# Two attention blocks in one kernel: sums of exponentials and divisors formed on column quarters, their inverses spread by way of DRAM

## The chip, the core and the metric

One core of a Trainium2 chip runs the whole program. The time is device time in microseconds (us), from the median of three runs: 2657.57 before the change (2656.48 to 2659.49). The profile is of one execution; in it the engines are PE (TensorE, matrix products), DVE (VectorE), ACT (ScalarE), POOL (GpSimd) and SP (which only issues transfers).

## What is computed

The input x has 8 images of 512 channels and 4096 pixels (64 x 64), all in float32. Two attention blocks follow each other.

Block 0, for each image:

```
f = Wf x + bf                      (64 x 4096)
g = pool2x2(Wg x + bg)             (64 x 1024)
v = pool2x2(Wh x + bh)             (256 x 1024)
s = f^T g ; beta = softmax(s)      (4096 x 1024, along the 1024)
o = v beta^T                       (256 x 4096)
x1 = gamma (Wv o + bv) + x
```

Block 1, on x1:

```
q = delu(Wq x1 + bq), k = delu(Wk x1 + bk)      (64 x 4096 each)
delu(z) = 10 relu(z) + exp(10 min(z, 0))
KV = k (Wv1 x1 + bv1)^T                         (64 x 512)
norm[n] = 1 / sum_d q[d, n] (sum_n k[d, n] + 1e-10)
out = x1 + gamma1 (KV^T q) norm
```

Two divisors matter here. The softmax of block 0 divides column n of the exponentials by their sum over 1024 rows. Block 1 divides column n of q by `norm`'s sum. Both are one number per pixel, while the data that they divide has pixels along the free dimension and something else on the 128 partitions. So the inverse is needed as a row that stands on every partition.

## The kernel before

Pixels are taken in chunks of 512 columns (`CH`), 8 per image, 64 in all (`TOTAL`). The function `step(s)` handles chunk s of the attention, and along with it work of other chunks, in three strands:

- A, for chunk a = s + 9: the products fg (L259) and, in a scheme of seven instead of eight partial products, H (L303), with pooling on DVE. POOL forms the sums of x that H needs (L292 to L295) and DVE the results.
- The attention of chunk s: M (L484, seven products with the exponentials E), N (L547, the output projection, added into the chunk of x called xb), and pk (L593, the features q and k of block 1). For chunk s + 1 the step computes the scores s (L394), their exponentials on ACT (L398), the sums over them on DVE (L432 to L437), the total (L441), its inverse (L446) and the normalized E (L460).
- C, for the image before (`b_c`), on pairs of chunks: `normalize` forms the divisors pd (L770), inverts them (L774) and multiplies q by the inverse (L777); `finish` forms pa (L795), copies it to y on ACT (L798), and POOL issues a transfer that adds y to the output in DRAM (L801). Two pa groups of 1 MB make up a pair. `normalize` runs on steps with j = 0, 1, 3, 5 of an image, `finish` on odd ones.

The order of the work on every engine is written by hand. Each piece is entered with `at(t, function, ...)`, t being a place within the step on a scale of about 41; the pieces are sorted by t and their instructions issued in that order on each engine's queue (`manual_schedule`). A place is not a time: an engine runs its queue in order as fast as its waits allow.

The total of the exponentials is a product with a matrix of ones: all 128 partitions of the result hold the same row of 512 sums. DVE inverts all of it. pd is made in the same way with the matrix kb, whose two diagonal blocks of 64 x 64 hold the sum of k in each row, so that partitions 0 to 63 hold the divisors of one chunk of the pair and partitions 64 to 127 those of the other.

PSUM is used as 8 banks that go round (`bank`), SBUF scratch as 7 buffers (`scratch`). A product enters PSUM in two matmul instructions[...].

A check runs alongside: `look` (L450, L451) sums the totals and inverses into chk; at the end DVE compares them with a limit and every engine reads the outcome. If it failed, the program would run once more in a general form; in these runs it does not.

SP issues the loads of x (L212, L224), the stores of xb (L574), the transposing transfers of v, x and k (u and uv; L358, L648, L630), and at the end the loads and stores of the last image, which takes another path for C.

Of the kernel before, what the change touches and what calls it, by code (L numbers as in the profile page):

```python
# [36 lines left out]
F32 = mybir.dt.float32  # L37
U16 = mybir.dt.uint16
AF = mybir.ActivationFunctionType
ALU = mybir.AluOpType  # L40
AX = mybir.AxisListType

PARAM = 10.0
EPS = 1e-10
P = 128
CH = 512
SAFE = 1e27

# [2 lines left out]
def tile_two_attention_blocks(  # L51
# [21 lines left out]
    nc = tc.nc  # L73
    B, C, H, W = x.shape
    N = H * W
    D = WfT.shape[1]
    CV = WhT.shape[1]
    KT = C // P
    VT = CV // P
    NCHUNK = N // CH  # L80
    M = N // 4
    MT = M // P
    NT = CH // P
    TOTAL = B * NCHUNK
    HN = CH // 2
    xr = x.rearrange("b (k p) h w -> b p k (h w)", p=P)
    outr = out.rearrange("b (k p) h w -> b p k (h w)", p=P)
    wv1r = wvT.rearrange("(k p) o -> p k o", p=P)

    const = ctx.enter_context(tc.tile_pool(name="const", bufs=1))  # L90
# [23 lines left out]
    for e in range(2):  # L114
        nc.scalar.dma_start(out=b_kq[e * D : (e + 1) * D, e : e + 1], in_=bk.rearrange("(p o) -> p o", o=1))
        nc.scalar.dma_start(
            out=b_kq[(1 - e) * D : (2 - e) * D, e : e + 1], in_=bq.rearrange("(p o) -> p o", o=1)
# [6 lines left out]
    ident = const.tile([P, P], F32, name="ident")  # L124
# [4 lines left out]
    ones = const.tile([P, P], F32, name="ones")  # L129
    nc.gpsimd.memset(ones, 1.0)  # L130

    kk = const.tile([P, CH], F32, name="kk")

    kb = const.tile([P, P], F32, name="kb")
# [28 lines left out]
    chk = const.tile([P, 2, TOTAL], F32, name="chk")  # L163

    def half(e):
        return slice(e * D, (e + 1) * D)

    def run(ctx, general):
# [6 lines left out]
        work1 = ctx.enter_context(tc.tile_pool(name="work1", bufs=1))  # L175
        work = ctx.enter_context(tc.tile_pool(name="work", bufs=2))
        temp = ctx.enter_context(tc.tile_pool(name="temp", bufs=7))
        turned = ctx.enter_context(tc.tile_pool(name="turned", bufs=1))
        small = ctx.enter_context(tc.tile_pool(name="small", bufs=4))
        psum = ctx.enter_context(tc.tile_pool(name="psum", bufs=8, space=bass.MemoryType.PSUM))  # L180

        def bank(name):
            return psum.tile([P, CH], F32, tag="m", name=name)

        def scratch(name):
            return temp.tile([P, CH], F32, tag="t", name=name)

# [38 lines left out]
        st = {}  # L226
        fgs, fs, vps = {}, {}, {}

        th, hs, es, sums, totals, rtots, te, os_, to, ns = ({} for _ in range(10))
        pxs, x_last, stored, late = [], {}, {}, {}  # L230
        kTs, xTs, pks, qq, halves, turned_halves = ({} for _ in range(6))

# [195 lines left out]
        def sum_of_e(s, m):  # L428
# [6 lines left out]
            else:  # L435
                r = sums[s]
                nc.vector.tensor_tensor(r[:, 0, :], r[:, 0, :], r[:, 1, :], ALU.add)  # L437

        def total(s):
            pt = totals[s] = bank(f"tot_{s}")  # L440
            nc.tensor.matmul(pt, ones, sums[s][:, 0, :], start=True, stop=True)  # L441

        def invert(s):

            rtots[s] = bank(f"rtot_{s}")
            nc.vector.reciprocal(rtots[s], totals[s])  # L446

        def look(s):
            pt = totals[s]
            nc.scalar.activation(pt, pt, AF.Copy, accum_out=chk[:, 0, s : s + 1])  # L450
            nc.scalar.activation(pt, rtots[s], AF.Copy, accum_out=chk[:, 1, s : s + 1])  # L451

        def block(s, i, j):

# [309 lines left out]
        def normalize(pair, at, t, t_invert, t_out):  # L764

            m = {}

            def product():
                m["pd"] = bank(f"pd_{pair}")
                nc.tensor.matmul(m["pd"], kb, qq[pair], start=True, stop=True)  # L770

            def inversion():
                m["rn"] = scratch(f"rn_{pair}")
                nc.vector.reciprocal(m["rn"], m["pd"])  # L774

            def out():
                nc.vector.tensor_tensor(qq[pair], qq[pair], m["rn"], ALU.mult)  # L777

            at(t, product)
            at(t_invert, inversion)  # L780
            at(t_out, out)

        def finish(pair, ks, at, t):

            b, jp = divmod(pair, NCHUNK // 2)
            m = {}

            def product():
                kv = st[b]["kv"]
                y = m["y"] = yc.tile([P, 2, 2, CH], F32, tag="y", name=f"y_{pair}_{ks[0]}")  # L790
                for i, k in enumerate(ks):
                    for e in range(2):
                        pa = bank(f"pa_{pair}_{k}_{e}")
                        hf = half(1 - e)
                        nc.tensor.matmul(  # L795
                            pa, kv[hf, bass.ts(k, P)], qq[pair][hf, :], start=True, stop=True
                        )
                        nc.scalar.copy(y[:, i, e, :], pa)  # L798

            def out():  # L800
                nc.gpsimd.dma_start(  # L801
                    out=outr[b, :, ks[0] : ks[0] + 2, bass.ts(jp, 2 * CH)],
                    in_=m["y"].rearrange("p k e n -> p k (e n)"), accum_op=ALU.add,
                )

            at(t, product)
            at(t + 3.4, out)


        def place(s, *tiles):  # L810
# [82 lines left out]
        def step(s):  # L893
            here, after = 0 <= s < TOTAL, 0 <= s + 1 < TOTAL
            a = s + LEAD
# [3 lines left out]
            pair = (b_c * NCHUNK + j) // 2  # L899
            work = []  # L900

            def at(t, fn, *args):
                work.append((t, len(work), fn, args))
# [50 lines left out]
                    turn_G(b_c, at, 19.5)  # L954
                    make_KV(b_c, at, 21.4, 30.0)
            if c_here and here and j == 0:
                normalize(pair, at, 5.6, 6.9, 13.2)
            if c_here and here and j % 2 == 1 and j < NCHUNK - 1:
                normalize(pair + 1, at, 3.5, 4.9, 4.95)
            if c_here and here and j % 2 == 1:  # L960
                finish(pair, (0, 1), at, 9.2)
                finish(pair, (2, 3), at, 10.9)
            if 0 <= a < TOTAL:
                a_h(a, at, 19.7, 29.1, 38.2 if here else 36.9, 38.4 if here else 37.8)

# [17 lines left out]
            if after:  # L983
                n = s + 1
                if here:
                    at(5.7, weigh_two, n, 0)
                    at(7.5, weigh_two, n, 2)
                    for m, t in ((2, 9.3), (4, 10.6), (6, 11.8), (8, 13.1)):
                        at(t, sum_of_e, n, m)

                if not here:
                    t, t_invert = 21.2, 21.25
                elif s == 0:
                    t, t_invert = 21.2, 22.6
                else:
                    t, t_invert = 16.1 if j % 2 == 1 and c_here else 17.85, 18.0
                at(t, total, n)
                at(t_invert, invert, n)
                if not general:
                    at(max(21.5, t_invert + 0.1), look, n)  # L1000
                at(24.3, normalize_block, n, 0, 1)
                at(26.0, normalize_block, n, 0, 0)
                at(27.3, normalize_block, n, 1, 1)
                at(29.2, normalize_block, n, 1, 0)
                at(33.6, sums_of_e, n, 1)
                at(36.0, sums_of_e, n, 2)
# [65 lines left out]
        for s in range(-LEAD, TOTAL + 1):  # L1072
            step(s)
# [5 lines left out]
    with ExitStack() as stack, tc.manual_schedule(engines=ENGINES):  # L1079
        run(stack, general=False)  # L1080

    least = const.tile([1, 1], F32, name="least")
    good = const.tile([1, 2 * TOTAL], F32, name="good")
    nc.vector.tensor_scalar(good, chk[0:1].rearrange("p c s -> p (c s)"), SAFE, None, ALU.is_lt)
    nc.vector.tensor_reduce(least, good, AX.X, ALU.min)
    bad = const.tile([1, 1], mybir.dt.int32, name="bad")
    nc.vector.tensor_scalar(bad, least, 0.5, None, ALU.is_lt)
    again = nc.values_load(bad, min_val=0, max_val=1, skip_runtime_bounds_check_because="0 or 1")
    with tc.If(again > 0):
        with ExitStack() as stack, tc.manual_schedule(engines=ENGINES):  # L1090
            run(stack, general=True)
# [37 lines left out]
```

## Time and profile before

| what | value |
|---|---|
| median of three runs | 2657.57 us |
| the profiled execution | 2656.62 us, span 2654.5 us, granted clock 0.994 |
| total L441: matmul instructions | 128, 66.1 us busy |
| divisors pd L770: matmul instructions | 56, 29.3 us busy |
| DVE reciprocal L446, 128 x 512 | 64, mean 3365 ns |
| DVE reciprocal L774, 128 x 512 | 28, mean 3351 ns |
| accumulating transfers L801 | 56 of 1 MB, 8.3 to 17.6 us to landing, median 11.4 |
| from total to total in the middle of an image | 39.3 and 40.2 us in turn (pa and pd stand in the longer one; on odd steps the total stands one M product earlier) |

The page gives busy time of each engine as a share of the span. A matmul's own duration includes its way through the array, so the time that it costs is read from start to start of neighbours in the timeline. An idle time stands with the group that ended it, and the entry behind the arrow names what it waited for. "Landing" is the time from a transfer's issue to its completion.

### The profile page before, as it was taken

What the parts mean: (1) busy time and instruction counts of PE and PEld (TensorE: products, weight loads), DVE (VectorE), ACT (ScalarE), POOL (GpSimd) and SP (SyncE); (2) the same over time, 40 slices, a digit from 0 to 9 for tenths busy, and PEclk for the clock granted to TensorE, in tenths of its full rate; (3) what the DMA queues carried; (4) which work ended last, traced back from release to release, by engine and by line L of the source; (5) the groups of instructions that cost most, each with busy time, mean ns of one, the idle gap of its engine ahead of it and who ended that gap; (6) DMA issues with size and microseconds to landing.
All of it is one profiled execution on the core that took longest, in us unless ns stands there. A gap on an engine that the chain in (4) does not pass through costs nothing.

```text
span 2654.5 us, 30415 instructions
## 1 busy us (share of the span) xinstructions
PE 2606.4 (98%) x10650; PEld 1798.1 (68%) x10650; DVE 2136.8 (80%) x2990; ACT 1593.2 (60%) x2670; POOL 763.5 (29%) x610
## 2 busy tenths in 40 slices
PE   8899999999999999999999999999999999999996
PEld 6577666667667667667667676666676676666663
DVE  5788879878888878887888888888788788798873
ACT  3365566566566566575675665666665656756661
POOL 4422323322322323223333223323223232221112
PEclk9999999999999999999999999999999999999998
DMA  5143455465555565655664654756555656455657
GB/s 172 49 134 89 115 135 149 104 164 134 133 157 118 142 167 118 164 133 116 152 162 121 155 125 123 180 116 151 141 118 158 155 119 159 117 138 138 154 144 256
DMA packets 465363, 369.91 MB, mean 139 GB/s; under 512 B 339888, under 2 KB 340400, under 8 KB 465200
## 3 DMA queue, kind: packets, MB, share of 16 engines
q1 hardware_dynamic: 444816, 307.16, 42.6%
q0 software_dynamic: 15232, 58.72, 12.0%
q10 hardware_dynamic: 5152, 1.97, 0.3%
q8 instruction: 87, 1.43, 0.2%
q14 instruction: 76, 0.62, 0.1%
HBM read 151.92 MB, written 134.22 MB: 108 GB/s over the span
## 4 chain that ended last, share of the span: by engine, by line
PE 87%; DVE 6%; DMA 1%; issue 1%; ACT 1%; POOL 0%; SPq 0%; DVEq 0%; POOLq 0%; ACTq 0%
PE M L484 27%; PE N L547 14%; PE H L303 11%; PE s L394 8%; PE pk L593 7%; PE fg L259 7%; PE pg L687 4%; PE pa L795 3%; PE tot L441 2%; PE pkv L752 1%; PE pd L770 1%; DMA xb<-in_x_dram 1%; DVE T L469 1%; DVE T L466 1%; DVE r L434 0%
## 5 line engine op out<-in xcount | busy, mean ns | idle before, releaser
L560 POOL TENSOR_TENSOR xb<-xb,n 128x512 f32<-128x512 f32 x192 | 246.7, 1285 | 553.3 <-ACT n L557 504.2
L484 PEld LDWEIGHTS M<-T,S 128*128 128x128 f32 x1536 | 286.5, 190 | 114.3 <-issue 29.2
L557 ACT ACTIVATE n<-N,gb_v 128x256 f32<-128x256 f32 x384 | 161.2, 471 | 334.1 <-PE N L547 333.2
L484 PE MATMUL M<-T,S 128*128 128x256 f32 x1536 | 358.7, 383 | 0.0
L655 ACT COPY xT<-u 128x1024 uint16<-128x1024 uint16 x252 | 328.2, 1353 | 1.4
L460 DVE TENSOR_TENSOR E<-E,rtot 128x1024 f32<-128x1024 f32 x256 | 305.2, 1214 | 3.8 <-issue 1.6
L642 ACT COPY w<-xb 128x1024 uint16<-128x1024 uint16 x252 | 244.8, 1042 | 81.8 <-DVE xb L563 81.8
L398 ACT ACTIVATE E<-s 128x512 f32<-128x512 f32 x512 | 256.1, 615 | 48.3 <-PE s L394 40.6
L446 DVE RECIPROCAL rtot<-tot 128x512 f32<-128x512 f32 x64 | 215.3, 3365 | 49.4 <-PE tot L441 49.4
L547 PE MATMUL N<-to,w_v 128*128 128x256 f32 x1024 | 243.6, 381 | 3.2 <-ACT n L557 3.0
L563 DVE TENSOR_TENSOR xb<-xb,N 128x512 f32<-128x512 f32 x256 | 175.0, 684 | 84.2 <-POOL xb L560 81.9
L394 PE MATMUL s<-f,g 64*128 64x512 f32 x1024 | 238.1, 602 | 1.9 <-DVE o L493 1.9
L593 PE MATMUL pk<-xb,w_kqk 128*128 128x512 f32 x512 | 231.8, 595 | 8.0 <-DVE xb L568 8.0
L634 POOL COPY kT<-uk 128x512 uint16<-128x512 uint16 x56 | 53.1, 949 | 620.6 <-DMA uk<-wk 620.6
L484 PE MATMUL M<-E,vT 128*128 128x256 f32 x1024 | 231.5, 379 | 0.0
L450 ACT ACTIVATE tot<-tot 128x512 f32<-128x512 f32 x64 | 37.7, 589 | 320.0 <-DVE rtot L446 319.9
L547 PEld LDWEIGHTS N<-to,w_v 128*128 128x128 f32 x1024 | 194.3, 191 | 30.8 <-ACT n L557 4.4
L484 PEld LDWEIGHTS M<-E,vT 128*128 128x128 f32 x1024 | 194.6, 190 | 29.4 <-issue 1.9
L259 PE MATMUL fg<-xa,w_fg 128*128 128x512 f32 x472 | 213.9, 596 | 0.0
L547 PE MATMUL N<-o,w_v 128*128 128x256 f32 x768 | 187.7, 380 | 1.9 <-ACT n L557 1.9
L547 PEld LDWEIGHTS N<-o,w_v 128*128 128x128 f32 x768 | 145.1, 190 | 54.8 <-issue 24.2
L394 PEld LDWEIGHTS s<-f,g 64*128 64x128 f32 x1024 | 94.7, 186 | 116.5 <-issue 90.6
(149 smaller groups left out, 4647.8 us busy)
## 6 DMA issues: line engine op xcount, KB each, us to landing
xb<-in_x_dram SPq DMA_DIRECT2D x64, 1024.0 KB, 5.7
out_dram<-xb SPq DMA_DIRECT2D x64, 1024.0 KB, 5.3
xa<-in_x_dram SPq DMA_DIRECT2D x59, 1024.0 KB, 7.4
out_dram<-y POOLq DMA_DIRECT2D x56, 1024.0 KB, 11.4
w_v<-in_L_conv_wv_dram SPq DMA_DIRECT2D x8, 1024.0 KB, 8.1
x_early<-in_x_dram SPq DMA_DIRECT2D x4, 1024.0 KB, 5.7
u<-w SPq DMA_TRANSPOSE x252, 3.3
x<-out_dram SPq DMA_DIRECT2D x12, 256.0 KB, 10.7
```

What stands on the lines that cost most here:

```text
L259: nc.tensor.matmul(fg, w_fg[:, k, :], x_a[a][:, k, :], start=(k == 0), stop=(k == KT - 1))
L303: nc.tensor.matmul(m[i], w_h7[i][:, k, :], th[a][i][:, k, :], start=(k == 0), stop=(k == hk - 1))
L394: nc.tensor.matmul(sc[e], g[half(e), i, :], fs[s][half(e), :], start=True, stop=True)
L398: nc.scalar.activation(es[s][:, 2 * i + e, :], sc[e], AF.Exp)
L446: nc.vector.reciprocal(rtots[s], totals[s])
L460: nc.vector.tensor_tensor(b, b, r, ALU.mult)
L484: nc.tensor.matmul(m[i], v7[i][:, k, :], te[s][i][:, k, :], start=(k == 0), stop=(k == hm - 1))
L547: nc.tensor.matmul(a[:, k, :], w_v7[i][:, bass.ts(k, P)], b, start=not more and k == 0, stop=True, skip_group_check=more or k > 0,)
L560: nc.gpsimd.tensor_tensor(of_x(*ij), of_x(*ij), u, ALU.add)
L593: nc.tensor.matmul(pk, w_kqk[:, i, e * D : (e + 2) * D], x_b[s][:, i, :], start=(i == 0), stop=(i == KT - 1),)
L642: nc.scalar.copy(w, x_b[s][:, k, :].bitcast(U16).rearrange("p (n h) -> p h n", h=2))
L655: nc.scalar.copy(v[:, k], u)
```

## The change

- `total` for s from 2 to 55 uses 32 columns of the ones for each of four column quarters of 128. Each quarter's sums land on their own 32 partitions of one PSUM tile of 128 x 128. DVE inverts that tile into SBUF (`rq`).
- `spread_inverses` sends one partition of each quarter to a row of DRAM and loads that row back, repeated on all 128 partitions; `keep_inverses` has ACT copy it into a PSUM bank, which the normalization reads as before. The first two chunks and those of the last image keep the full product.
- `product` of `normalize` uses 32 columns of kb around its middle, so that each quarter's 32 partitions hold 16 rows of each chunk's divisors. `inversion` inverts 128 x 128, sends eight rows to DRAM and loads them back on 64 partitions each, in two transfers.
- Both inverted tiles share the tag `rq` with one buffer. The transfers are SP's; they stand ahead of the transposing transfer of v (18.7) on its queue.
- The places of C: product, inversion and multiplication at 12.65, 13.7 and 30.9. The accumulating transfers go to 22.6 and 22.7, behind POOL's sums of x. On step 55 (`a == TOTAL`) both groups of pa stand at 21.4 and 22.3, behind the last M and ahead of N.
- On step 55 the total stands at 21.2, inverted at 22.6; on later even steps at 19.55 and 19.6.
- The check at the end covers all 128 partitions of chk, with a transpose and a second reduction.

```diff
@@ -43,6 +43,7 @@
 PARAM = 10.0
 EPS = 1e-10
 P = 128
+QP = 32
 CH = 512
 SAFE = 1e27
 
@@ -177,6 +178,7 @@
         temp = ctx.enter_context(tc.tile_pool(name="temp", bufs=7))
         turned = ctx.enter_context(tc.tile_pool(name="turned", bufs=1))
         small = ctx.enter_context(tc.tile_pool(name="small", bufs=4))
+        rows = ctx.enter_context(tc.tile_pool(name="rows", bufs=2, space=bass.MemoryType.DRAM))
         psum = ctx.enter_context(tc.tile_pool(name="psum", bufs=8, space=bass.MemoryType.PSUM))
 
         def bank(name):
@@ -226,7 +228,7 @@
         st = {}
         fgs, fs, vps = {}, {}, {}
 
-        th, hs, es, sums, totals, rtots, te, os_, to, ns = ({} for _ in range(10))
+        th, hs, es, sums, totals, rq, rtots, te, os_, to = ({} for _ in range(10))
         pxs, x_last, stored, late = [], {}, {}, {}
         kTs, xTs, pks, qq, halves, turned_halves = ({} for _ in range(6))
 
@@ -436,19 +438,45 @@
                 r = sums[s]
                 nc.vector.tensor_tensor(r[:, 0, :], r[:, 0, :], r[:, 1, :], ALU.add)
 
+        def by_quarters(s):
+
+            return 1 < s < TOTAL - NCHUNK
+
         def total(s):
-            pt = totals[s] = bank(f"tot_{s}")
-            nc.tensor.matmul(pt, ones, sums[s][:, 0, :], start=True, stop=True)
+            if not by_quarters(s):
+                totals[s] = bank(f"tot_{s}")
+                nc.tensor.matmul(totals[s], ones, sums[s][:, 0, :], start=True, stop=True)
+                return
+
+            pt = totals[s] = bank(f"tot_{s}")[:, 0:P]
+            for i in range(NT):
+                nc.tensor.matmul(
+                    pt[bass.ts(i, QP), :], ones[:, 0:QP], sums[s][:, 0, bass.ts(i, P)],
+                    start=True, stop=True,
+                )
 
         def invert(s):
-
-            rtots[s] = bank(f"rtot_{s}")
-            nc.vector.reciprocal(rtots[s], totals[s])
+            if by_quarters(s):
+                rq[s] = work1.tile([P, P], F32, tag="rq", name=f"rq_{s}")
+            else:
+                rq[s] = rtots[s] = bank(f"rtot_{s}")
+            nc.vector.reciprocal(rq[s], totals[s])
+
+        def spread_inverses(s):
+
+            d = rows.tile([NT, P], F32, tag="rd", name=f"rd_{s}")
+            nc.sync.dma_start(out=d, in_=rq[s][0:P:QP, :])
+            u = rtots[s] = scratch(f"rb_{s}")
+            nc.sync.dma_start(out=u, in_=d.rearrange("(o i) n -> o (i n)", o=1).to_broadcast([P, CH]))
+
+        def keep_inverses(s):
+            u, rtots[s] = rtots[s], bank(f"rtot_{s}")
+            nc.scalar.copy(rtots[s], u)
 
         def look(s):
             pt = totals[s]
             nc.scalar.activation(pt, pt, AF.Copy, accum_out=chk[:, 0, s : s + 1])
-            nc.scalar.activation(pt, rtots[s], AF.Copy, accum_out=chk[:, 1, s : s + 1])
+            nc.scalar.activation(pt, rq[s], AF.Copy, accum_out=chk[:, 1, s : s + 1])
 
         def block(s, i, j):
 
@@ -766,12 +794,26 @@
             m = {}
 
             def product():
-                m["pd"] = bank(f"pd_{pair}")
-                nc.tensor.matmul(m["pd"], kb, qq[pair], start=True, stop=True)
+
+                pd = m["pd"] = bank(f"pd_{pair}")[:, 0:P]
+                for i in range(NT):
+                    nc.tensor.matmul(
+                        pd[bass.ts(i, QP), :], kb[:, D - QP // 2 : D + QP // 2],
+                        qq[pair][:, bass.ts(i, P)], start=True, stop=True,
+                    )
 
             def inversion():
-                m["rn"] = scratch(f"rn_{pair}")
-                nc.vector.reciprocal(m["rn"], m["pd"])
+                rd = work1.tile([P, P], F32, tag="rq", name=f"rq_pd_{pair}")
+                nc.vector.reciprocal(rd, m["pd"])
+                d = rows.tile([2 * NT, P], F32, tag="rn", name=f"rn_{pair}_row")
+                nc.sync.dma_start(out=d, in_=rd[0 : P : QP // 2, :])
+                rn = m["rn"] = scratch(f"rn_{pair}")
+                for e in range(2):
+                    row = d.rearrange("(i e) n -> e i n", e=2)[e : e + 1]
+                    nc.sync.dma_start(
+                        out=rn[half(e)].rearrange("p (i n) -> p i n", n=P),
+                        in_=row.to_broadcast([D, NT, P]),
+                    )
 
             def out():
                 nc.vector.tensor_tensor(qq[pair], qq[pair], m["rn"], ALU.mult)
@@ -780,7 +822,7 @@
             at(t_invert, inversion)
             at(t_out, out)
 
-        def finish(pair, ks, at, t):
+        def finish(pair, ks, at, t, t_out):
 
             b, jp = divmod(pair, NCHUNK // 2)
             m = {}
@@ -804,7 +846,7 @@
                 )
 
             at(t, product)
-            at(t + 3.4, out)
+            at(t_out, out)
 
 
         def place(s, *tiles):
@@ -954,12 +996,14 @@
                     turn_G(b_c, at, 19.5)
                     make_KV(b_c, at, 21.4, 30.0)
             if c_here and here and j == 0:
-                normalize(pair, at, 5.6, 6.9, 13.2)
+                normalize(pair, at, 12.65, 13.7, 30.9)
             if c_here and here and j % 2 == 1 and j < NCHUNK - 1:
-                normalize(pair + 1, at, 3.5, 4.9, 4.95)
+                normalize(pair + 1, at, 12.65, 13.7, 30.9)
             if c_here and here and j % 2 == 1:
-                finish(pair, (0, 1), at, 9.2)
-                finish(pair, (2, 3), at, 10.9)
+
+                cover = a == TOTAL
+                finish(pair, (0, 1), at, 21.4 if cover else 9.2, 24.9 if cover else 22.6)
+                finish(pair, (2, 3), at, 22.3 if cover else 10.9, 25.8 if cover else 22.7)
             if 0 <= a < TOTAL:
                 a_h(a, at, 19.7, 29.1, 38.2 if here else 36.9, 38.4 if here else 37.8)
 
@@ -990,12 +1034,17 @@
 
                 if not here:
                     t, t_invert = 21.2, 21.25
-                elif s == 0:
+                elif s == 0 or a == TOTAL:
                     t, t_invert = 21.2, 22.6
+                elif a > TOTAL and s % 2 == 0:
+                    t, t_invert = 19.55, 19.6
                 else:
                     t, t_invert = 16.1 if j % 2 == 1 and c_here else 17.85, 18.0
                 at(t, total, n)
                 at(t_invert, invert, n)
+                if by_quarters(n):
+                    at(18.01, spread_inverses, n)
+                    at(23.0, keep_inverses, n)
                 if not general:
                     at(max(21.5, t_invert + 0.1), look, n)
                 at(24.3, normalize_block, n, 0, 1)
@@ -1079,12 +1128,16 @@
     with ExitStack() as stack, tc.manual_schedule(engines=ENGINES):
         run(stack, general=False)
 
-    least = const.tile([1, 1], F32, name="least")
-    good = const.tile([1, 2 * TOTAL], F32, name="good")
-    nc.vector.tensor_scalar(good, chk[0:1].rearrange("p c s -> p (c s)"), SAFE, None, ALU.is_lt)
+    least = const.tile([P, 1], F32, name="least")
+    good = const.tile([P, 2 * TOTAL], F32, name="good")
+    nc.vector.tensor_scalar(good, chk.rearrange("p c s -> p (c s)"), SAFE, None, ALU.is_lt)
     nc.vector.tensor_reduce(least, good, AX.X, ALU.min)
+    with tc.tile_pool(name="row", bufs=1, space=bass.MemoryType.PSUM) as last:
+        row = last.tile([1, P], F32, name="row")
+        nc.tensor.transpose(row, least, ident)
+        nc.vector.tensor_reduce(least[0:1], row, AX.X, ALU.min)
     bad = const.tile([1, 1], mybir.dt.int32, name="bad")
-    nc.vector.tensor_scalar(bad, least, 0.5, None, ALU.is_lt)
+    nc.vector.tensor_scalar(bad, least[0:1], 0.5, None, ALU.is_lt)
     again = nc.values_load(bad, min_val=0, max_val=1, skip_runtime_bounds_check_because="0 or 1")
     with tc.If(again > 0):
         with ExitStack() as stack, tc.manual_schedule(engines=ENGINES):
```

## The prediction

> **What bounds the kernel now.** The page's busy shares and its chain of work come first, since they say which engine must be relieved.
>
> ```profile
> PE 2606.4 (98%) x10650; PEld 1798.1 (68%) x10650; DVE 2136.8 (80%) x2990; ACT 1593.2 (60%) x2670; POOL 763.5 (29%) x610
> PE 87%; DVE 6%; DMA 1%; issue 1%; ACT 1%; POOL 0%; SPq 0%; DVEq 0%; POOLq 0%; ACTq 0%
> ```
>
> TensorE is the bound. Relief on DVE, ACT or a queue is worth nothing by itself; only TensorE time that disappears counts, against TensorE waits that appear. Next, TensorE's timeline over one step without C (start us, length us, group):
>
> ```profile
> 1225.58 1.89 PE L484 MATMUL M<-E,S 128*128 128x256 f32 x8
> 1227.40 3.70 PE L394 MATMUL s<-f,g 64*128 64x512 f32 x16
> 1231.04 1.94 PE L687 MATMUL pg<-xT,kT 128*64 128x512 f32 x8
> 1232.90 3.72 PE L484 MATMUL M<-T,S 128*128 128x256 f32 x16
> 1236.46 1.02 PE L441 MATMUL tot<-r,ones 128*128 128x512 f32 x2
> 1237.32 1.89 PE L484 MATMUL M<-T,S 128*128 128x256 f32 x8
> 1239.05 1.89 PE L484 MATMUL M<-T,vT 128*128 128x256 f32 x8
> 1240.77 3.60 PE L259 MATMUL fg<-xa,w_fg 128*128 128x512 f32 x8
> ```
>
> Starts follow each other without a gap, and they price everything. A product is two matmul instructions. Eight of 256 columns take 1.73 us from start to start (1237.32 to 1239.05). The total takes 0.86 (1236.46 to 1237.32), so a 128-column quarter of one of its instructions is 0.107. Eight pg instructions of 512 columns in array tiles of 128*64 take only 1.86 instead of 8 x 0.43: two column tiles run side by side. A change of tile shape shows too: M from 1225.58 is due to end at 1227.31, s starts at 1227.40, so 0.09 of draining, and the first weights can't be loaded ahead, which costs about 0.10 for 128 columns (16 M instructions take 3.56 here, 3.46 without a change before them) and by the same comparison 0.05 for pg's 64.
>
> The waits around the two divisors, in the answers on `pd` and `tot` (us, times), and the first step of an image:
>
> ```profile
>   DVE kb L723: 9.0, 13
> ...
>   DVE r L437: 4.8, 5
> ...
> 1060.64 1.89 PE L484 MATMUL M<-E,S 128*128 128x256 f32 x8
> 1063.05 1.13 PE L770 MATMUL pd<-qq,kb 128*128 128x512 f32 x2 [0.51 <-DVE kb L723]
> ```
>
> That `pd` starts 0.67 late (M is due to end at 1062.37), once in each image. Last, what shall take DVE's long reciprocal's place, DVE's timeline in the same step:
>
> ```profile
> 1237.52 3.37 DVE L446 RECIPROCAL rtot<-tot 128x512 f32<-128x512 f32 x1 [1.28 <-PE tot L441]
> 1244.16 1.21 DVE L460 TENSOR_TENSOR E<-E,rtot 128x1024 f32<-128x1024 f32 x1
> 1245.40 0.69 DVE L236 TENSOR_REDUCE gp<-fg 64x128 f32<-64x512 f32 x1
> ```
>
> The normalization of E begins at 1244.16; that is the time to meet.
>
> **What the Trainium skill says.** "TensorEngine Tiling (Array Packing)", Available Configurations and Key Properties: 128×32 gives four independent tiles, and a change of tiling mode drains TensorE. The trace agrees for two tiles (pg) and shows the drain (0.09); it has no 128×32. "TensorE: Matmul & The Clock Gate", Measured speedup vs the span model, gives 3.07× for four row tiles and 2.38× for three column tiles, short of ideal; pg here is nearly ideal. "DMA: Bandwidth & Descriptors", Two DMAs through the same engine are not ordered: a transfer that reads what another wrote must wait for its semaphore. So the way by DRAM costs two whole landings in series. The same page's Issuing engines are not separate DMA queues: SP's and POOL's transfers share the 16 engines. The trace agrees: `uv`, sent behind two accumulating transfers, lands after up to 12.2 us, else 2.4 at best.
>
> **The change, part by part.** *Sums of exponentials (54 steps, s = 2 to 55).* Removed: 0.86 of TensorE. Added between two M products: drain 0.09; first weights of 32 columns, extrapolated from 0.10 and 0.05 to 0.03; two passes, each between 0.107 (four tiles fully side by side) and 0.14 (3.07 of 4), I take 0.12; starts staggered 0.02; on the way back 0.10 drain and 0.10 weights. Sum 0.58, saved 0.28; 54 x 0.28 = 15.1 us.
>
> *C's divisors (28 pairs).* Removed: 0.86, plus the late starts, 7 x 0.67 = 4.7, or 0.17 each. Added: the product now stands behind pg and before M, where the way back to 128*128 is paid already: 0.10 + 0.03 + 0.24 + 0.02 = 0.39. Saved 0.64; 28 x 0.64 = 17.9.
>
> *Late total of the last image (19.55 on even steps after 56) and no pd reciprocal before the sums.* The late sums held `tot` up for 4.8 in all; three even steps and one odd one of that stage make 2.9 of it (gaps before `tot` of about 0.82 and 0.46). Gone: 2.9.
>
> *C once amid M and N (step 55).* It moves 3.5 us of pa, behind M and a full-width total. N there is delayed by pa, and its own waits on ACT's eviction (0.93) and on DVE before pk (1.34) follow N's products. So I give it nothing.
>
> *DVE.* A reciprocal of 512 columns is 3.37 and one of 16 columns 0.26 (L850), so 128 columns make 0.96: about 2.4 saved 82 times, worth nothing while TensorE is the bound.
>
> *ACT.* One copy of 0.59 is added per step, and the two looks shrink. ACT idles 3.00 us before N's first eviction at 1245.33. If its input is late, that eviction and f queue behind it.
>
> *The way by DRAM.* Landings: a 1 MB store takes 4.3 at best, a 256 KB one 2.0, which extrapolates to 1.3 for a row of 2 KB; bounds 1.3 to 2.0. A 256 KB load takes 3.0 at best. In the step above: quarters end about 1237.05, reciprocal to 1238.05, row out 1239.5 to 1240.2, broadcast in 1242.6 to 1243.2, ACT's copy to 1243.9 at the latest, so E starts between 1243.3 and 1243.9, no later than now. What is late next if it slips: E, then gp L236, then f on ACT (which waits for gp), then the second eviction, which has 0.35 to spare and N's next product 0.7 more. So 1245.2, or 1244.9 with TensorE 0.3 earlier, still costs nothing. In a C step the chain is longer: pd's inversion, its row out, two half broadcasts on SP (0.5 to issue each), and only then the total's row; both reciprocals share one buffer, so the second waits for the first row's landing. With the step at 1193.44 (pg) I get E at 1204.7 to 1205.9, against 1205.29 now and 1207.6 as the last harmless time. Behind these transfers SP holds only `uv`, about 7 us later, and its reader at 1251.43 has time. qq's multiplication moves to DVE's idle of 1.19 at 1214.
>
> *Accumulating transfers.* They are issued about 10 us later, behind POOL's sums (end 1204.4) and before its next addition (1208.59): two issues of 1.19 fit. From first issue to second landing takes 13.7 now, so they would end about 1218.1, over the start of the u transposes (1216.9) whose reader has 1.7 to spare. Bounds: 0, and about 1 us in 28 steps; I take 0.
>
> *The end.* The check over 128 partitions adds a transpose and a reduction behind the last products; the stores on SP run 10 us longer. Nothing.
>
> The sum: 15.1 + 17.9 + 2.9 = 35.9. The profiled execution took 2656.6, so 2620.7; the median is 0.95 higher: **2622**.
>
> **The rivals.** *Slips a little, still faster:* row out and broadcast together take about 6.2 instead of 4.3 to 5.0, 0.3 over what is harmless, in 54 steps: 2622 + 16 = 2638. For it: such a pair stands nowhere in this trace. *Slower, the way by DRAM becomes the bound:* E may start at 1244.9, which is a pair of 5.9; every us beyond costs TensorE one us in 54 steps, so from 6.6 the gain is gone. At 7.4 it is 2622 + 81 = 2703. For it: a 1 MB load takes 5.7 and `uv` up to 12.2 amid accumulating traffic, which in C steps starts just when the broadcast should land. Against it: at that time the queues are otherwise empty (xb lands about 1236.6, the next transposes come after 1216.9 or 1254). *Column quarters don't run side by side:* a total then takes 8 x 0.109 + 0.34 = 1.21, so 54 x 0.35 = 19 lost, pd even: 2657.6 + 19 - 2.9 = 2674. Against it: pg's two tiles.
>
> **How the numbers follow.** Forecast 2622 (own range 2610 to 2633): 0.68. Small slip: 0.16. Way by DRAM bound: 0.09. No overlap: 0.05. A balance that ends within 0.2% (5.3 us, about what a measurement can tell): 0.02. Hence faster 0.84, same 0.02, slower 0.14. Below 2608 I leave 0.04; the range reaches up over the small slip to 2652 and leaves out both slower cases.
>
> **What would show it.** `tot` and `pd` as 8 instructions of 128*32, with four starts within 0.03 and 0.5 to 0.6 from M to M; no idle before `pd`; the steps shorter by 0.3, with pd by 0.9; reciprocals of 0.96; `rd` landing in under 2.0 and `rb` in about 3; E's start no later than now; no N or pk waiting on ACT or DVE amid images. Wrong would be: n or f on ACT idle until a DMA, or quarters one behind another.

## The result, and the profile after

The changed kernel takes 2638.19 us (median of 4 runs, 2636.13 to 2640.14), the one before in the same comparison 2658.53: ratio 0.9924, 95% interval 0.9907 to 0.9941. It is faster by 20.3 us (16 to 25); 2622, faster by 35.9, was forecast. The mechanism held and its size didn't: some 16 us of the expected gain are missing.

Busy time and the chain of work of the page after:

```profile
PE 2582.3 (98%) x11143; PEld 1775.0 (67%) x11143; DVE 1955.6 (74%) x2991; ACT 1590.0 (60%) x2724; POOL 761.0 (29%) x610
PE 86%; DVE 5%; DMA 2%; ACT 1%; issue 1%; POOL 0%; DVEq 0%; POOLq 0%; SPq 0%; ACTq 0%
```

TensorE is still the bound; its busy time fell by 24.1. Among the small shares DMA went from 1% to 2%; the load of the spread row (`rb`), which is new, makes 0.5% of the span. TensorE's timeline in the step that the prediction used:

```profile
1220.36 3.72 PE L512 MATMUL M<-T,S 128*128 128x256 f32 x16
1224.02 0.42 PE L453 MATMUL tot<-r,ones 128*32 128x128 f32 x8
1224.37 1.99 PE L512 MATMUL M<-T,S 128*128 128x256 f32 x8
1226.20 1.89 PE L512 MATMUL M<-T,vT 128*128 128x256 f32 x8
```

Eight instructions of 128*32 take 0.35 from start to start (1224.02 to 1224.37). One behind the other they would take 8 x 0.107 = 0.86, and the four starts of a pass lie within 0.02: four column tiles do run side by side. The way in costs 0.10 (3.66 before the total, after 3.56 in the same place before) and the way back 0.10 (1.83 to the next M, 1.73 without). From M to M the total was 0.86 and is now 0.55, a saving of 0.31 for the 0.28 forecast. VectorE, in the same step:

```profile
1224.51 0.96 DVE L463 RECIPROCAL rq<-tot 128x128 f32<-128x128 f32 x1 [0.85 <-PE tot L453]
...
1231.05 1.22 DVE L488 TENSOR_TENSOR E<-E,rtot 128x1024 f32<-128x1024 f32 x1 [1.07 <-ACT rtot L474]
```

The reciprocal takes 0.96, as forecast. E now waits for the way by DRAM (1.07), but starts 0.31 ahead of N's first product (1231.36), so nothing on TensorE waits for it. Next, TensorE in the first step of an image, where `pd` came late before:

```profile
1056.03 1.94 PE L715 MATMUL pg<-xT,kT 128*64 128x512 f32 x8
1057.89 0.43 PE L800 MATMUL pd<-qq,kb 128*32 128x128 f32 x8
1058.25 3.72 PE L512 MATMUL M<-T,S 128*128 128x256 f32 x16
```

`pd` costs 0.36 here and starts on time.

### The profile page after: what moved, and what is told of

Its sections match the earlier page's. It is cut to its first block, busy times and chain, and to the rows that moved or that the text cites. A ratio compares the mean times of both kernels' runs of the same rounds, so it can differ in the third digit from the quotient of the medians.

```text
span 2634.2 us, 31842 instructions
## 1 busy us (share of the span) xinstructions
PE 2582.3 (98%) x11143; PEld 1775.0 (67%) x11143; DVE 1955.6 (74%) x2991; ACT 1590.0 (60%) x2724; POOL 761.0 (29%) x610
## 4 chain that ended last, share of the span: by engine, by line
PE 86%; DVE 5%; DMA 2%; ACT 1%; issue 1%; POOL 0%; DVEq 0%; POOLq 0%; SPq 0%; ACTq 0%
PE M L512 28%; PE N L575 13%; PE H L305 12%; PE pk L621 8%; PE s L396 8%; PE fg L261 7%; PE pg L715 4%; PE pa L837 4%; PE pkv L780 1%; DVE E L488 1%; PE tot L453 1%; DMA rb<-rd 1%; DVE r L436 1%; DVE xb L591 0%; DMA x<-out_dram 0%
## 5 line engine op out<-in xcount | busy, mean ns | idle before, releaser
L512 PEld LDWEIGHTS M<-T,S 128*128 128x128 f32 x1536 | 282.1, 190 | 80.1 <-ACT E L400 24.1
L621 PE MATMUL pk<-xb,w_kqk 128*128 128x512 f32 x512 | 232.5, 597 | 11.3 <-DVE xb L596 9.4
L294 POOL TENSOR_TENSOR tha<-xa 128x512 f32<-128x512 f32 x59 | 81.4, 1379 | 531.0 <-PE M L512 508.6
L434 DVE TENSOR_TENSOR r<-E 128x1024 f32<-128x1024 f32 x64 | 78.4, 1226 | 191.6 <-ACT E L400 191.6
L474 ACT COPY rtot<-rb 128x512 f32<-128x512 f32 x54 | 31.8, 589 | 239.5 <-DMA rb<-rd 239.5
```

The costliest lines, as they stand in the source:

```text
L512: nc.tensor.matmul(m[i], v7[i][:, k, :], te[s][i][:, k, :], start=(k == 0), stop=(k == hm - 1))
L621: nc.tensor.matmul(pk, w_kqk[:, i, e * D : (e + 2) * D], x_b[s][:, i, :], start=(i == 0), stop=(i == KT - 1),)
```

## Where the rest went

Two measures carry all that follows, both read from starts in the trace. The first is the time from one step's first pk to the next step's, compared with the kernel before, added up by image. A row runs from an image's first pk to the next image's, so it holds the first step of the next image and not its own (the stretch ahead of the first pk differs by -1.4 to +3.8 us from one execution to another and is left out; the last row includes the end of the run):

| image | after | e11 | e3 | e4 |
|---|---|---|---|---|
| 1 | -2.4 | -3.4 | -3.7 | -3.7 |
| 2 | -4.5 | -4.9 | -5.3 | -5.3 |
| 3 | -4.2 | -4.8 | -5.2 | -5.2 |
| 4 | -4.3 | -4.8 | -5.2 | -5.2 |
| 5 | -2.1 | -4.1 | -5.2 | -5.2 |
| 6 | -4.7 | -4.8 | -5.2 | -5.2 |
| 7, with step 55 | -0.1 | -0.5 | -0.6 | -3.7 |
| 8 | +1.7 | +2.9 | +2.5 | -0.7 |
| sum | -20.7 | -24.4 | -28.0 | -34.2 |

By the unit savings a row of images 2 to 6 should show 8 x 0.31 + 4 x 0.50 + 0.77 = 5.25 (0.50 for each `pd`, 0.77 for the late start), and the row of image 1, which holds one `pd`, 3.75. "After" stays short of it in each of them, and loses 4.4 over the last ten intervals, that is from step 55 on.

The second is by how much E's normalization starts after N's first product in the same step (minus: before it; the last image is left out):

| step | before | after | e3 | e11 | e7 | e8 |
|---|---|---|---|---|---|---|
| even, without pa | -0.05 | -0.4 to 0 | -0.5 to -0.1 | -0.4 to 0 | +1.5 to 2.2 | -0.4 to 0 |
| first of an image | -0.34 | +1.5 to 3.3 | -1.3 to -0.4 | +1.0 to 2.2 | +0.7 to 2.2 | -1.2 to -0.6 |
| j = 1, 3, 5 | -1.32 | -0.6 to +0.4 | -1.5 to -1.3 | -1.5 to -0.7 | -0.4 to +0.4 | +3.1 to 3.8 |

Three theories follow from this. **Order on SP:** in the first step of an image the row of the sums stands behind pd's row and its two broadcasts. **Step 55:** C amid M and N costs what it was to cost nothing. **Late total:** in the last image the total at 19.55 loses more than it saves. The rival for each is the prediction's own statement, and for the first, another cause of the same waits.

## Experiments

### The loads of pd's inverse behind the sums' (e3), and its two halves (e10, e11)

```diff
-                rd = work1.tile([P, P], F32, tag="rq", name=f"rq_pd_{pair}")
+                rd = work1.tile([P, P], F32, tag="rqd", name=f"rq_pd_{pair}")
                 nc.vector.reciprocal(rd, m["pd"])
                 d = rows.tile([2 * NT, P], F32, tag="rn", name=f"rn_{pair}_row")
                 nc.sync.dma_start(out=d, in_=rd[0 : P : QP // 2, :])
+                m["d"] = d
+
+            def spread_rn():
+                d = m["d"]
                 rn = m["rn"] = scratch(f"rn_{pair}")
                 for e in range(2):
...
             at(t_invert, inversion)
+            at(18.02, spread_rn)
```

e10 is the new tag alone, e11 the rest alone.

> The inverse of pd gets a buffer of its own, and the two loads of rn are issued behind rd and rb instead of ahead of them. Theory A (in an image's first step the row of the sums stands behind pd's way by DRAM, E starts 16.2 us after pg instead of 12.6 and TensorE loses about 1.0): E of that step starts 2 to 3 us earlier and 6 us go in seven first steps (5 to 7), near 2632. Theory B (the waits of that step, N, H and pk, have another cause than E): E starts earlier and the time stays.

> The changed kernel with a buffer of its own for pd's inverse and nothing else: half of the edit that put the loads of rn behind rb. Theory A (the row of the sums is held up by the order on SP, not by the shared buffer): VectorE no longer waits 1.9 for the first row's landing in an image's first step, but rd is issued as late as now; less than 1.5 gained of the ten. Theory B (the shared buffer is the cause): 6 or more gained, near 2632.

> The other half: the loads of rn behind rd and rb, both inverses still in one buffer. Theory A (order on SP): in an image's first step rd follows the reciprocal at once and lands in 1.65, not 2.1 or more, so E starts 0.8 earlier; in the steps with j = 1, 3, 5, where the second reciprocal hardly waits for the first row, E comes back to 1.5 before N. 5 to 8 of the ten gained, 2630 to 2633. Theory B (both halves are needed): less than 3 gained.

Measured: e3 2628.06, ratio 0.9884 (0.9869 to 0.9899); e10 2637.18, 0.9921 (0.9909 to 0.9934); e11 2632.13, 0.9899 (0.9885 to 0.9913). The first step of an image can be compared directly, since pg starts at 1056.03 in both executions. SP's queue, VectorE and TensorE of the changed kernel, one timeline after the other:

```profile
1062.44 0.58 SPq L809 DMA_DIRECT2D rn_row<-rq_pd  x1
1064.54 1.31 SPq L813 DMA_DIRECT2D rn<-rn_row  x2
1065.95 0.56 SPq L468 DMA_DIRECT2D rd<-rq  x1
1068.02 0.35 SPq L470 DMA_DIRECT2D rb<-rd  x1
```

```profile
1064.60 0.96 DVE L463 RECIPROCAL rq<-tot 128x128 f32<-128x128 f32 x1 [1.91 <-DMA rn_row<-rq_pd]
...
1072.21 1.22 DVE L488 TENSOR_TENSOR E<-E,rtot 128x1024 f32<-128x1024 f32 x1 [2.97 <-ACT rtot L474]
```

```profile
1081.46 3.67 PE L621 MATMUL pk<-xb,w_kqk 128*128 128x512 f32 x8 [0.25 <-issue]
```

and of e3, whose first row goes out at 1062.46:

```profile
1063.60 0.49 SPq L468 DMA_DIRECT2D rd<-rq  x1
1065.21 0.34 SPq L470 DMA_DIRECT2D rb<-rd  x1
1065.66 1.31 SPq L817 DMA_DIRECT2D rn<-rn_row  x2
```

```profile
1069.74 1.22 DVE L488 TENSOR_TENSOR E<-E,rtot 128x1024 f32<-128x1024 f32 x1 [1.67 <-ACT rtot L474]
```

```profile
1080.50 3.60 PE L621 MATMUL pk<-xb,w_kqk 128*128 128x512 f32 x8
```

In the changed kernel pd's row goes out at 1062.44; VectorE waits until it has landed, since both inverses share one buffer (1.91), and SP waits for the same landing and then spends 1.31 issuing two loads that VectorE uses only at 1079.09. So rd goes out at 1065.95 (1063.60 in e3), E starts 2.07 after N's first product (1070.14), and pk comes 0.96 later than in e3, where E starts 0.40 ahead of it. Theory A of e3 stands in the trace: 7.6 us in images 1 to 6, each 0.5 to 3.1. The medians put it at 10, with an uncertainty that covers 7.6. Of the halves the order on SP is the larger: 4.5 in these images, and its interval ends below the changed kernel's 0.9924. The buffer alone leaves E where it was (+1.7 to 3.2); its median is 1.0 lower, which its interval doesn't tell from nothing, and added up over the same images its intervals gain nothing (they lose 0.2). Once the order is right, the buffer gives the rest. Image 5 of the changed kernel lost more than the others; most of that went with the order too, and why it was this image stays open.

### Step 55 and the late totals (e1, e2, e4)

```diff
-                cover = a == TOTAL
+                cover = False
...
-                elif s == 0 or a == TOTAL:
+                elif s == 0:
```

for e1, and for e2

```diff
-                elif a > TOTAL and s % 2 == 0:
-                    t, t_invert = 19.55, 19.6
```

e4 has both and e3's edit.

> Step 55 is put back as an ordinary odd step: both groups of pa at 9.2 and 10.9, their transfers at 22.6 and 22.7, the (full-width) total at 16.1 and its inverse at 18.0. Theory A (the move of C amid M and N costs what the two TensorE intervals of that step gained, 2.03 + 0.73 us): about 2.8 us less than the changed kernel, so near 2635.4, and N and pk of that step without the waits of 1.36 and 1.58. Theory B (the prediction's: worth nothing): no difference.

> The total of the last image's even steps is put back to 17.85, its inverse to 18.0. Theory A (late reciprocals push kk, the copy of q and N's eviction back): in each of three steps the wait of tot for r, 0.9, comes back, and 1.4 around N (0.89 at its longest wait) goes, so 1.5 us less than the changed kernel, near 2636.7. Theory B (the prediction's term): 2.9 us more, 2641.

> The three edits before together. Theory A: the gains add up, 2.8 + 1.5 + 6 = 10.3 less than the changed kernel, near 2628. Theory B (one wait stands behind the other): less than 7.

Measured: e1 2633.95, 0.9912 (0.9898 to 0.9925); e2 2633.87, 0.9916 (0.9902 to 0.9929); e4 2625.23, 0.9873 (0.9858 to 0.9888). The intervals of e1 and e2 overlap the changed kernel's, so the traces decide. Step 55 of the changed kernel, on TensorE, VectorE and ACT in turn:

```profile
2301.40 1.02 PE L448 MATMUL tot<-r,ones 128*128 128x512 f32 x2
2302.35 3.70 PE L837 MATMUL pa<-qq,kv 64*128 64x512 f32 x16
...
2310.21 3.19 PE L575 MATMUL N<-to,w_v 128*128 128x256 f32 x12 [1.36 <-ACT n L585]
```

```profile
2304.62 3.37 DVE L463 RECIPROCAL rtot<-tot 128x512 f32<-128x512 f32 x1 [1.59 <-ACT y L840]
```

```profile
2308.02 0.58 ACT L478 ACTIVATE tot<-tot 128x512 f32<-128x512 f32 x1 [0.49 <-DVE rtot L463]
...
2309.33 0.83 ACT L585 ACTIVATE n<-N,gb_v 128x256 f32<-128x256 f32 x2
```

The total, still at full width here, starts at 2301.40; its inverse, behind a wait for ACT's copy of y, ends at 2307.99. The looks at both stand ahead of N's eviction on ACT's queue and take 1.3 more, so N's second part waits 1.36. In e4, where the step is an ordinary one, that part runs through:

```profile
2302.87 4.05 PE L575 MATMUL N<-to,w_v 128*128 128x256 f32 x16
```

Step for step, the intervals of steps 55 and 56 differ from the kernel before by +2.03 and +0.73 in the changed kernel, -0.01 and +2.30 in e1, +2.02 and -0.47 in e2, 0.00 and -0.30 in e4. The move costs 2.0 in its own interval, but where it is undone alone the late total of step 56 costs 2.6, and 1.2 beside it. So theory A of e1 names the right waits, but its sum of 2.8 fails: over both intervals 0.5 shows while the late totals stand, and 1.9 once they are gone (e2 against e4). The median of e1 is 4.2 lower than the changed kernel's, but its interval doesn't tell that from 0.5. An even step of the last image, first on ACT and then on TensorE, in the changed kernel:

```profile
2411.99 0.62 ACT L646 COPY qq<-kk 64x512 f32<-64x512 f32 x1 [2.47 <-DVE kk L640]
```

```profile
2413.39 1.13 PE L575 MATMUL N<-to,w_v 128*128 128x256 f32 x4 [0.72 <-ACT n L585]
```

The 0.90 that `tot` no longer waits is gone from the step, but the long reciprocal then stands 1.7 later against pk, ahead of E and kk on VectorE; the copy of q on ACT waits 2.47 for kk, N's eviction stands behind it, and N loses 1.4 in all. The same step in e2:

```profile
2398.53 1.10 PE L448 MATMUL tot<-r,ones 128*128 128x512 f32 x2 [0.65 <-DVE r L439]
...
2411.10 1.03 PE L575 MATMUL N<-to,w_v 128*128 128x256 f32 x4
```

The wait before `tot` is back, 0.65 of it idle, and the one before N is gone. By the intervals e2 gains 3.8 (1.2 at step 56, 2.6 in the last row), more than the 1.5 expected: step 56 and the last even step had not been counted. e4 shows images 2 to 6 at 5.2 or 5.3 and image 1 at 3.7, and its 2625.2 beats both kernels. Against the changed kernel it gains 13.5 by the table and 13.0 by the medians: the three gains add up, with step 55's at the 1.9 that it is worth beside e2 (alone it is 0.5).

### Each half alone (e5, e6)

e5 takes the kernel before and gives it only the totals by quarters; e6 only C's divisors, with C's new places. For e5, against the kernel after:

```diff
-                normalize(pair, at, 12.65, 13.7, 30.9)
+                normalize(pair, at, 5.6, 6.9, 13.2)
...
-                finish(pair, (0, 1), at, 21.4 if cover else 9.2, 24.9 if cover else 22.6)
-                finish(pair, (2, 3), at, 22.3 if cover else 10.9, 25.8 if cover else 22.7)
+                finish(pair, (0, 1), at, 21.4 if cover else 9.2, 24.9 if cover else 12.6)
+                finish(pair, (2, 3), at, 22.3 if cover else 10.9, 25.8 if cover else 14.3)
```

with the product and inversion of `normalize` as before and e1's and e2's edits; for e6 `by_quarters` returns False, with the same two edits.

> The kernel before with one part of the change: only the sums of exponentials by quarters (54 of them, with their way by DRAM and the check over 128 partitions); C's divisors, their reciprocals of 512 columns, places and transfers as before. Theory A (a product by quarters saves 0.31 wherever nothing waits for it): 54 x 0.31 = 16.7 less than before, near 2640.6, and E no later against N than before. Theory B (without C's new places the way by DRAM meets the accumulating transfers): less than 12 saved.

> The other part alone: C's divisors by quarters at their new places, transfers behind the sums of x; the totals at full width as before. Theory A: 28 x 0.50 for the product and 7 x 0.77 for the late start in an image's first step = 19.4 less than before, near 2638. Theory B (with the long reciprocal of the total behind pd's on VectorE, E gets late in steps with pd): less than 12 saved.

Measured: e5 2693.16, ratio 1.0138 (1.0120 to 1.0156), so 35 us slower than before; e6 2642.57, 0.9941 (0.9923 to 0.9959). e6 shows -0.50 for each `pd` but the last one, which gains nothing, and -1.27 to -1.32 in the first step of images 3 to 7, as expected; the first steps of images 2 and 8 gain only 0.7 and 0.3, the end loses 1.2, and the sum is 16.4 and not 19.4. e5 shows -0.31 in every step without C's transfers and up to +2.4 in those with them. In those steps E starts 2.7 to 3.5 after N. Neither of its theories had it lose, though theory B named the transfers.

### The accumulating transfers (e8), and the last image (e9)

On e4, the transfers at their old places (e8):

```diff
-                finish(pair, (0, 1), at, 21.4 if cover else 9.2, 24.9 if cover else 22.6)
-                finish(pair, (2, 3), at, 22.3 if cover else 10.9, 25.8 if cover else 22.7)
+                finish(pair, (0, 1), at, 21.4 if cover else 9.2, 24.9 if cover else 12.6)
+                finish(pair, (2, 3), at, 22.3 if cover else 10.9, 25.8 if cover else 14.3)
```

and, also on e4 alone, quarters for the last image's totals too (e9):

```diff
-            return 1 < s < TOTAL - NCHUNK
+            return 1 < s
```

> On the three edits together: the accumulating transfers are issued at 12.6 and 14.3 again, ahead of POOL's sums of x, as before the change. Theory A (their 2 MB then share the DMA engines with the rows and the loads that spread them): in steps with C rb takes 5 instead of 3.3, E starts 1.7 later against N, still not beyond N's start plus 1.0, so less than 10 slower. Theory B (they hold the rows up by whole landings, as a transposing transfer behind them takes up to 12): 27 steps lose 3 or more, over 80 slower.

> On the three edits together: the totals of the last image (56 to 63) by quarters as well, with their way by DRAM. Theory A (nothing waits for it): 8 x 0.31 = 2.5 less, near 2622.7. Theory B (on even steps of the last image the total stands 0.9 later, waiting for r, and E and behind it kk get 0.7 later than with the long reciprocal, then the copy of q and N's eviction as in the late totals): even steps gain nothing or lose up to 0.4, so between 1.5 less and 1 more.

Measured: e8 2686.11, 1.0102 (1.0084 to 1.0120), 61 more than e4; e9 2648.89, 0.9962 (0.9950 to 0.9974), 24 more. SP's queue and POOL in a step with C, in e4:

```profile
1186.69 0.49 SPq L468 DMA_DIRECT2D rd<-rq  x1
1188.30 0.34 SPq L470 DMA_DIRECT2D rb<-rd  x1
```

```profile
1191.81 2.40 POOL L848 DMA_DIRECT2D out_dram<-y  x2
```

in e8:

```profile
1209.58 0.49 SPq L468 DMA_DIRECT2D rd<-rq  x1
1214.76 0.34 SPq L470 DMA_DIRECT2D rb<-rd  x1
```

```profile
1204.32 1.19 POOL L848 DMA_DIRECT2D out_dram<-y  x1 [7.04 <-ACT y L845]
1206.28 1.19 POOL L848 DMA_DIRECT2D out_dram<-y  x1 [0.77 <-ACT y L845]
```

and SP's queue in e9, in the last image, where POOL issued its two transfers at 2366.54 and 2368.50:

```profile
2369.64 0.53 SPq L468 DMA_DIRECT2D rd<-rq  x1
2375.51 0.33 SPq L470 DMA_DIRECT2D rb<-rd  x1
```

rb is issued when rd has landed, so the gap between the two is the row's landing: 1.61 where the two megabytes follow, 5.18 and 5.87 where they are already on their way. rb then takes 4.2 to 5.7 and not 3.3. In e8 E starts 3.0 to 3.8 after N and an odd step with quarters of `pd` loses 2.0 in place of gaining 0.8. By the medians the loss is between the two theories of e8, nearer to theory B and with its mechanism: 23 steps (not 27) lose 2.2 to 3.2 each. The limit "N plus 1.0" was somewhat generous: 3.3 late costs 2.8, so it stands nearer to 0.5 in these steps. The Trainium skill states what they share in "DMA: Bandwidth & Descriptors", Issuing engines are not separate DMA queues (one set of 16 engines for all), and this case gives the price, a 2 KB row from 1.6 to 5.2 or more. In the last image POOL has no sums of x for the transfers to stand behind: they go at once, and e9, whose two theories both missed, fell into the same trap: four totals lose 4.8 to 6.0 each. So the limit in `by_quarters` that leaves the last image out is worth 24 us here.

### A longer way (e7)

```diff
             nc.sync.dma_start(out=d, in_=rq[s][0:P:QP, :])
+            d0, d = d, rows.tile([NT, P], F32, tag="rd2", name=f"rd2_{s}")
+            nc.sync.dma_start(out=d, in_=d0)
```

> On the three edits together: the row of inverted sums is copied once more from DRAM to DRAM before it is spread, which should lengthen the way by 1.7 to 2.0. Theory A (E may start up to 1.0 after N's first product; on even steps it starts 0.25 before it now, on odd ones 1.5): the even steps, about 30, lose 0.4 to 0.8 each and the odd ones nothing: 12 to 24 slower, 2637 to 2649. Theory B (every us of the way counts): 54 x 1.8 = 97 slower. Theory C (another 2 us are free): no difference.

Measured: 2676.92, ratio 1.0065 (1.0044 to 1.0086), 52 more than e4. The way is longer by 1.9 (rd and its copy take 3.5 to 4.0 in nearly all steps, against 1.65), even steps start E 1.5 to 2.2 after N and lose 0.7 to 1.2 each; that is theory A's part, some 24 us. The rest it had left out. Among the waits of the changed kernel there is

```profile
ACT vT L365 <- DMA uv<-wv: 1.1, 2, 0.9
```

and of e7

```profile
ACT vT L365 <- DMA uv<-wv: 39.7, 11, 5.7
```

(us, times, longest). SP issues `uv` behind rb. In steps 9 to 53 with accumulating transfers, 23 in all, e4 has `uv` go out 1.3 to 3.0 ahead of the first of them; e7 has it 0.2 to 0.7 behind it in 18. In ten of these 18 ACT's copy of v, with all of ACT behind it, waits 2.1 to 5.7 for `uv` (the eleventh wait stands at the start of the program, as in the changed kernel). The ten intervals at the end of these steps lose 2.0 to 5.3 against e4, 35 of the 57 that all intervals lose. Why the other eight don't wait stays open.

## Why the prediction was right, and where not

- **Sums of exponentials, 0.28 x 54 = 15.1:** right, 0.31 (16.7). The Trainium skill's 3.07 of 4, taken as one bound ("TensorE: Matmul & The Clock Gate", Measured speedup vs the span model), is for row tiles; here two full-width instructions took 0.86, and eight of 128 columns with both changes of tile shape 0.55.
- **Divisors, 17.9:** right. The product saves 0.50 for the 0.47 forecast, and by the unit savings the part is worth 28 x 0.50 + 7 x 0.77 = 19.4; e6, which has it alone, shows 16.4 in its trace.
- **Late total, "Gone: 2.9":** wrong in sign. The wait before `tot` went and a longer one before N came, since the reciprocal of 3.37 is still whole in this stage and kk, q and an eviction queue behind it: 3.8 us worse than the old place. The step priced the wait that it removed and did not follow what stands behind the moved reciprocal on VectorE.
- **C amid M and N, "I give it nothing":** wrong, 1.9 us with the late totals gone. It looked at N's old waits, and not at ACT's queue, where the looks at a late inverse stand ahead of N's eviction, nor at the inverse's own wait for the copies of y.
- **The way by DRAM:** right for the step without C (row 1.65, bounds 1.3 to 2.0; broadcast 3.3, taken as 3.0 or a little more; E 12.55 after pg, forecast 12.3 to 12.9). For the C step it was too early: 11.3 to 12.5 after pg by its sum, 12.6 to 13.6 measured with j = 1, 3, 5, since the row of the sums lands in 2.0 to 3.1 behind the two loads of rn. That is still ahead of the 14.2 that it called harmless, and costs little. Wrong by omission for the first step of an image: the C step worked out has pa ahead of pg, so VectorE has ended the sums of E before pg is there and pd's inversion follows soon; the first step has no pa, the inversion stands behind these sums, and its row goes out 6.4 after pg (3.6 in the step that follows, 1106.04 against 1102.47). E comes 15.6 to 17.4 after pg there. Together with the slips on odd steps that is 7.6 us.
- **Accumulating transfers, "I take 0":** right as the price of the move, and blind to its worth. The rival "the way by DRAM becomes the bound" named their traffic as the cause and put the end at 2703 with a pair of 7.4 in every step; with the transfers at their old places it is a pair of 10.3 in 23 steps, and 2686. So the rival's cause is that of the kernel without this part of the change.
- **The rival "slips a little", 2638:** its number was met by chance and its mechanism only partly. E is late in the six first steps that have quarters, not in 54, and 5.7 of the 13.3 lost have nothing to do with the way by DRAM. The main case, 2610 to 2633, was missed; the range up to 2652 held because it left room for a small slip.

The losses add up to 7.6 + 1.9 + 3.8 = 13.3, and e4, which is free of them, takes 2625.2; the forecast without its term of 2.9, which e4 leaves out, is 2625. That the two meet so closely is in part luck: the unit savings make 16.7 + 19.4 = 36.1 where the forecast had 33.0, and e4 gains 34.2 of it by the table and 32.1 by the medians.

## What to carry to other kernels

A broadcast by way of DRAM is two small transfers in series, and its length is set by what else is on the DMA engines: before it replaces work on an engine, find the bulk transfers issued in the same microseconds and put them behind it. On an issuing queue, what the critical path needs goes ahead of what can wait, even if it is ready later. A step that is moved in "each image" has to be worked out for each kind of step, the first one above all, and for the stage in which its usual neighbours are missing.

## What the runs showed of the hardware

- Four column tiles of 128*32 with 128 columns each, in two instructions per tile, take 0.35 from start to start, against 0.86 for the two instructions of a 128*128 product of 512 columns; the change of tile shape ahead of them and the one behind them cost 0.10 each.
- A row of 2 KB from SBUF to DRAM lands in 1.6 to 1.7 where nothing stands close ahead of it, in 2.0 to 3.1 with two broadcasts of 128 KB just ahead of it, in 5.2 to 6.4 behind two accumulating transfers of 1 MB: 3.6 to 4.8 more.
- A row repeated on 128 partitions (256 KB) lands in 3.0 to 3.7 in most steps, behind the accumulating transfers in 4.2 to 5.7.
- VectorE's reciprocal takes 0.96 for 128 columns and 3.37 for 512.
